# Sixteen-batch attention and FFN on one core: the down products of batches 13 and 14 computed one stage later

## The chip, the cores and the metric

The kernel runs on one core of a Trainium2 chip. The metric is the device time of one execution in microseconds (us); lower is better. TensorE is called PE here, VectorE DVE, ScalarE ACT, GpSimd POOL, and the queue of SyncE, which issues nearly all transfers, SP.

## The reference

For x of 16 batches, 512 tokens and 512 channels, in float32, one transformer layer with a layernorm ahead of and behind each half:

```python
x = x + layernorm(attention(layernorm(x), Wq, bq, Wk, bk, Wv, bv, Wo, bo))
x = x + layernorm(ffn(layernorm(x), gate_w, up_w, down_w, gate_s, up_s, down_s))

# attention: 32 heads of 16 channels, rotary turns, causal softmax
q, k, v = heads(x @ Wq.T + bq), heads(x @ Wk.T + bk), heads(x @ Wv.T + bv)
weights = softmax(where(causal, rope(q) @ rope(k).T / sqrt(16), -inf))
out = merge(weights @ v) @ Wo.T + bo

# ffn: 1408 inner channels, weights of -1, 0 and 1
g = (x @ gate_w.T) * gate_s
u = (x @ up_w.T) * up_s
out = ((silu(g) * u) @ down_w.T) * down_s
```

## The kernel before

**Stages.** The batches are handled one after another. A stage belongs to the attention of one batch b and has 8 groups of four heads with 6 steps each, 48 steps (`batches`, L910; `one_step`, L751). In every step PE computes scores of the current group (into the tile `st`, which ACT turns into weights `pt` with an exp, and POOL masks with an `affine_select`), and scores of the next group or the one after it (into the tiles `s`, from which DVE takes the maxima). Products of weights and values (`av`) follow in step 3 of a group and in step 0 of the next; their copy by ACT is `ot`. The tile `st` has one buffer in PSUM, `s` two, which is what one step fills. DVE turns the maxima round through PE (`pm`) and DMAs put them into `mx` (L615).

**What fills the steps.** Between these, each step takes a part of a list of other work. `dense` (L494) lists, for the next batch, the products of v, q and k, and for the batch before, the output product of the attention (`po`, `o_block`, L362), its two layernorms, and the transposes of the result (`px`, `turn`, L254). `ffn_list` (L706) lists the FFN of the batch before: 11 times a gate and an up product (`pg`, `pu`, L404), then for each of four blocks of 128 tokens a down product (`pd`, L429), and between these the first layernorm and transposes of the batch after the next. `merge` and `laid` (L468, L473) place follow-up work a given number of units behind a product; `run_list` (L693) spreads the list over the 48 steps by the units of its items (1 for a float32 product of 512 columns, 0.27 for one of the gate, up and down products, 0.15 for a transpose). So in stage 15 the list has the work of no next batch; L518 sets an item of 28 units that does nothing at its head. Each engine takes its instructions strictly in the order that the program writes them.

**Splits.** On the path that runs here (`self.exact`), the left operands of the gate, up and down products are parts of a float32 value, a rounded one and the rest, so each of these products comes twice. For the down product ACT copies four columns of blocks of `ht` into `hh`, and POOL computes the rest, `hl` (`split`, L458). Each has two buffers, and a down product of a block is 22 matmuls in three chunks (8, 8 and 6), each with a split of its own. In `ffn_list`, the split of chunk k of block tb + 1 is written behind chunk k of block tb, so its buffer is freed by the chunk that comes after it.

**The way of the heads.** When a group is done, `ot` goes to DRAM (`od`); after every second group, `sums` (L675) reads the sums and the values back (tiles `sum` and `oc`), DVE takes the reciprocal, it goes to DRAM (`rd`) and comes back repeated (tile `xr`), and POOL multiplies `oc` by it. `oc` has four buffers, one for each of the four pieces of 128 channels of a batch; `xr` has two, which also carry the residual x that `load_xr` (L390) reads.

**The end.** After stage 15 eight steps finish the attention (with no other work), and then L927 writes the rest of batch 15 in one piece: output product, layernorms, transposes, gate, up and down.

Of the kernel before, what the change touches and what calls it, by code (L numbers as in the profile page):

```python
# [18 lines left out]
P = 128  # L19
T = 512  # L20
C = 512
# [32 lines left out]
class Block:  # L54
# [15 lines left out]
    def __init__(self, tc, ctx, a):  # L70
        self.tc, self.a = tc, a
        nc = self.nc = tc.nc
        self.pe = InOrder(tc, nc.tensor)
        self.dve = InOrder(tc, nc.vector)
        self.act = InOrder(tc, nc.scalar)
        self.pool = InOrder(tc, nc.gpsimd)
        self.sp = InOrder(tc, nc.sync)
        self.B = a["x"].shape[0]
        self.F = a["wd"].shape[0]
        self.NF = self.F // P  # L80
        pool = lambda name, **k: ctx.enter_context(tc.tile_pool(name=name, **k))
        self.const = pool("const", bufs=1)
        self.work = pool("work", bufs=2)
        self.small = pool("small", bufs=5)
        self.dram = pool("dram", bufs=1, space=bass.MemoryType.DRAM)
        self.ps_s = pool("ps_s", bufs=2, space=bass.MemoryType.PSUM)
        self.ps_t = pool("ps_t", bufs=1, space=bass.MemoryType.PSUM)
        self.ps_av = pool("ps_av", bufs=1, space=bass.MemoryType.PSUM)
        self.ps_d = pool("ps_d", bufs=3, space=bass.MemoryType.PSUM)
        self.todo = defaultdict(list)  # L90
        self.step = 0
        self.exact = False
        for name in "xts xns xnts x1s x2ts ks qs mxs nms pts avs ots ocs rcs wts hts wfs yas xrs pieces".split():
            setattr(self, name, {})
        self.constants()
# [266 lines left out]
    def o_block(self, b, tb):  # L362

        st = {}

        def tail(p):
            x1 = st["x1"] = self.tile([P, C], "x1", bufs=4)
            self.dve.tensor_tensor(x1, p, self.row["bo"], ALU.add)
            st["mr"] = self.stats(x1)

        def rest_1():
            x1 = self.x1s[b, tb] = st["x1"]
            self.scaled(x1, x1, st["mr"])
            self.pool.tensor_tensor(x1, x1, self.xrs.pop((b, tb)), ALU.add)
            if tb + 2 < NB:
                self.load_xr(b, tb + 2)

        def rest_2():
            st["mr"] = self.stats(st["x1"])

        def rest_3():
            xn = self.tile([P, C], "xn", bufs=2)
            self.scaled(xn, st["x1"], st["mr"])
            self.xns[("f", b), tb] = xn

        return self.product(
            "po", NC, lambda c: self.ocs[b, c][:, ts(tb, P)], lambda c: self.wts[b, "o", c // 2][:, c % 2, :], tail
        ), rest_1, rest_2, rest_3
# [102 lines left out]
                waiting.remove(w)  # L491
        return out + [(0, w[1]) for w in waiting]

    def dense(self, b):  # L494


        L = []
        nxt, old = b + 1 < self.B, b >= 1
        o, bn = b - 1, b + 1
        do = lambda f, *args: L.append((0, lambda: f(*args)))  # L500

        def qk(name, c):
            items, rest, store = self.qk_block(bn, name, c)
            L.extend(items)
            self.merge(L, rest, 3)
            self.merge(L, store, 5.5)

        if nxt:
            for tb in range(NB):
                L += self.v_block(bn, tb)  # L510
            for c in range(NC):
                if c < 2:
                    do(self.load_w, o, "o", c)
                qk("q", c)
                if c % 2:
                    do(self.load_w, bn, "k", c // 2)
        elif b < self.B:
            L.append((28 * MM, lambda: None))  # L518
        if not nxt:
            for half in range(2):  # L520
                do(self.load_w, o, "o", half)
        later = []
        if old:
            do(self.load_xr, o, 0)
            do(self.load_xr, o, 1)
            for tb in range(NB):
                items, *rests = self.o_block(o, tb)
                L += items
                for r, k in zip(rests, (3.5, 6.5, 9.5)):
                    if r is rests[2] and tb >= 2:  # L530
                        later.append(r)
                    else:
                        self.merge(L, r, k, ("f", tb))
        for c in range(NC):
            if old:
                if c < 2:
                    do(self.load_wf, o, c)
                L.append(("need", ("f", c)))
                L += self.turn(self.xns, ("f", o), c, self.xnts, "xntf")
                if c < 2:  # L540
                    self.merge(L, later[c], 5, ("f", c + 2))
            if nxt:
                qk("k", c)
        return L
# [102 lines left out]
    def values(self, n, third):  # L647
        b, g = divmod(n, NG)
        if third == 0:
            self.avs[n] = self.ps_av.tile([P, T], FP, tag="av", name="av")  # L650
        av = self.avs[n]
        for kb, at, w in ST_SETS[third]:
            for j in range(4):
                h = 4 * g + j
                pt = self.pts[n, third, j // 2]
                pt = pt[:, j // 2, T // 2 * (j % 2) :] if third == 2 else pt[:, j % 2, :]
                self.pe.matmul(
                    av[32 * j : 32 * j + 32, T - w : T],
                    self.v17[b % 2][:, kb, h * W : h * W + 32],
                    pt[:, at : at + w],  # L660
                    start=(kb == 0),
                    stop=(third == 2),
                )
        for pair in range(2):
            del self.pts[n, third, pair]
        if third == 2:
            del self.ks[n], self.qs[n], self.mxs[n]
            ot = self.tile([P, T], "ot", bufs=1)
            self.act.copy(ot, self.avs.pop(n))
            i = (b % 2) * NC + g // 2  # L670
            self.later(1, lambda: self.sp.dma_start(out=self.od[i][P * (g % 2) : P * (g % 2) + P, :], in_=ot))
            if g % 2:
                self.later(2, self.sums, b, g // 2)

    def sums(self, b, c):  # L675
        i = (b % 2) * NC + c
# [26 lines left out]
                i += 1  # L703
            yield

    def ffn_list(self, o, nxt2):  # L706

        L = []
        do = lambda f, *args: L.append((0, lambda: f(*args)))
        NK = (self.NF + 3) // 4  # L710
        for f in range(self.NF if o is not None else 0):
            if f + 2 < self.NF:
                do(self.load_wf, o, f + 2)
            L += self.gate_up(o, f)
            if self.exact and (f % 4 == 3 or f == self.NF - 1):
                do(self.split, o, 0, f // 4)
            if nxt2 is not None:
                if 3 <= f < 7:
                    do(self.load_w, nxt2, "vq"[(f - 3) // 2], (f - 3) % 2)
                elif 7 <= f < 9:  # L720
                    do(self.load_x, nxt2, f - 7)
        if o is None:
            for tb in range(2):
                do(self.load_x, nxt2, tb)
            for k in range(4):
                do(self.load_w, nxt2, "vq"[k // 2], k % 2)
        for tb in range(NB):
            if nxt2 is not None:
                st = {}

# [2 lines left out]

                do(first)
                self.merge(L, lambda st=st: st["rest"](), 4, ("a", tb))
            if o is not None:
                items, rest, store = self.down(o, tb)
                if self.exact and tb + 1 < NB:
                    for k in range(NK):
                        L += items[8 * k : 8 * k + 8]  # L740
                        do(self.split, o, tb + 1, k)
                else:
                    L += items
                self.merge(L, rest, 4)
                self.merge(L, store, 8)
            if nxt2 is not None:
                L.append(("need", ("a", tb)))
                L += self.turn(self.xns, ("a", nxt2), tb, self.xnts, "xnta")
        return L

    def one_step(self, work, n, i):  # L751
        for f, args in self.todo.pop(self.step, []):
# [157 lines left out]
    def batches(self):  # L910
# [5 lines left out]
                self.one_step(work, n, i)  # L916
        for b in range(B):
            if b:
                L = self.dense(b) + self.ffn_list(b - 1, b + 2 if b + 2 < B else None)
                work = self.run_list(L, NG * STEPS)  # L920
            for g in range(NG):
                for i in range(STEPS):
                    self.one_step(work, b * NG + g, i)

        for i in range(STEPS + 2):
            self.one_step(iter(()), B * NG + i // STEPS, i % STEPS)
        for _, f in self.laid(self.dense(B) + self.ffn_list(B - 1, None)):  # L927
            f()


# [59 lines left out]
```

## Time and profile before

| | |
|---|---|
| time, median of 3 runs | 3273.52 us (3272.84 to 3274.5) |
| the profiled execution, its own time | 3268.2 us |
| its span, first to last instruction | 3266.5 us |
| mean granted PE clock | 0.973 |
| matmuls recorded | 21258 |
| bytes read and written in HBM | 345.79 MB, 125.30 MB |
| stage 13, from the last `ot` of batch 12 to the last of batch 13 | 191.3 us |
| stage 14, the same of batches 13 and 14 | 197.5 us |
| stage 15, the same of batches 14 and 15 | 188.4 us |
| from there to the first gate product of batch 15 | 49.2 us |
| from there to the end | 76.4 us |

How to read it: the profile is of one execution. Its busy times are sums over the instructions of an engine; matmuls overlap, so that the sum of their durations says less than the distance of their starts. The clock is the share of full speed that PE was granted. A wait is written as the waiting engine and group, an arrow, and what ended the wait, then us in total, times, and the longest. A stage is measured from the `ot` copy of the last group of one batch to that of the next, where the records show a stage's start and end best.

### The profile page before, as it was taken

What the parts mean: (1) busy time and instruction counts of PE and PEld (TensorE: products, weight loads), DVE (VectorE), ACT (ScalarE), POOL (GpSimd) and SP (SyncE); (2) the same over time, 40 slices, a digit from 0 to 9 for tenths busy, and PEclk for the clock granted to TensorE, in tenths of its full rate; (3) what the DMA queues carried; (4) which work ended last, traced back from release to release, by engine and by line L of the source; (5) the groups of instructions that cost most, each with busy time, mean ns of one, the idle gap of its engine ahead of it and who ended that gap; (6) DMA issues with size and microseconds to landing.
All of it is one profiled execution on the core that took longest, in us unless ns stands there. A gap on an engine that the chain in (4) does not pass through costs nothing. (4 is left out here: it accounts for less than half of the span.)

```text
span 3266.5 us, 59287 instructions
## 1 busy us (share of the span) xinstructions
PE 3110.4 (95%) x21258; PEld 1751.5 (54%) x21258; DVE 1888.5 (58%) x5911; ACT 1543.1 (47%) x2243; POOL 1383.4 (42%) x1933
## 2 busy tenths in 40 slices
PE   6889999999999999999999999999999999997868
PEld 2334655646455564645556464555646555463536
DVE  5455656565565656556565665656656565655522
ACT  5354545454454545445454545545454554543332
POOL 4143345453444545344454434445442544533142
PEclk9889999999999999999999999999999999997988
DMA  6454525345352534535244453535445353433321
GB/s 250 162 165 151 192 96 177 128 147 167 127 194 91 178 130 148 171 125 190 98 163 135 153 176 124 181 105 163 137 150 167 127 182 107 146 116 104 105 79 66
DMA packets 227441, 471.41 MB, mean 144 GB/s; under 512 B 40976, under 2 KB 45072, under 8 KB 226704
## 3 DMA queue, kind: packets, MB, share of 16 engines
q1 hardware_dynamic: 226704, 466.47, 42.9%
q8 instruction: 170, 2.79, 0.3%
q10 hardware_dynamic: 432, 1.05, 0.1%
q14 instruction: 135, 1.11, 0.1%
HBM read 345.79 MB, written 125.30 MB: 144 GB/s over the span
## 5 line engine op out<-in xcount | busy, mean ns | idle before, releaser
L49 DVE CUSTOM_DVE_ANT_0 s<-s,mask 128x512 f32<-128x512 f32 (+1 forms) x2034 | 974.8, 510 | 715.1 <-PE s L49 534.8
L49 ACT ACTIVATE pt<-st 128x1024 f32<-128x1024 f32 (+1 forms) x768 | 677.0, 881 | 753.3 <-PE st L49 742.7
L49 POOL TENSOR_SCALAR_AFFINE_SELECT pt<-pt 128x256 f32<-128x256 f32 (+1 forms) x768 | 392.7, 511 | 1200.9 <-ACT pt L49 1198.4
L49 PEld LDWEIGHTS st<-q,kh 32*128 32x128 f32 x2048 | 193.2, 185 | 473.7 <-issue 229.9
L49 PE MATMUL st<-q,kh 32*128 32x512 f32 (+3 forms) x2048 | 414.9, 401 | 31.3 <-ACT pt L49 29.8
L49 PE MATMUL s<-kh,q 32*128 32x512 f32 (+1 forms) x2034 | 415.9, 402 | 15.8 <-DVE nm L49 8.1
L49 PE MATMUL s<-kl,q 32*128 32x512 f32 (+1 forms) x2034 | 344.8, 324 | 11.5 <-DMA kl<-kd 11.4
L49 PE MATMUL st<-mx,one 2*128 2x512 f32 (+3 forms) x2048 | 335.9, 324 | 5.3 <-DMA mx<-nml 5.3
L49 PE MATMUL av<-pt,v 128*32 128x512 f32 (+3 forms) x4096 | 338.7, 449 | 0.0
L49 PE MATMUL st<-q,kl 32*128 32x512 f32 (+3 forms) x2048 | 336.5, 325 | 0.0
L49 POOL TENSOR_TENSOR hl<-ht,hh 128x512 fp32r<-128x512 f32 (+1 forms) x192 | 229.7, 1196 | 199.8 <-ACT hh L49 191.2
L49 DVE DVE_READ_ACCUMULATOR2_ANT nm<- 128x1 f32 x2048 | 289.4, 141 | 0.0
L49 PE MATMUL pd<-wd,hl 128*128 128x512 f32 x704 | 286.8, 407 | 2.0 <-POOL hl L49 2.0
L49 PE MATMUL pg<-xntf,wf 128*128 128x512 f32 x704 | 287.0, 408 | 1.3 <-ACT xntf L49 1.3
L49 PE MATMUL pd<-wd,hh 128*128 128x512 f32 x704 | 287.9, 409 | 0.0
L49 PE MATMUL pu<-xntf,wf 128*128 128x512 f32 x704 | 284.2, 404 | 0.0
L49 PE MATMUL pu<-xntfl,wf 128*128 128x512 f32 x704 | 284.0, 403 | 0.0
L49 PE MATMUL pg<-xntfl,wf 128*128 128x512 f32 x704 | 281.0, 399 | 0.0
L49 PE MATMUL po<-w,oc 128*128 128x512 f32 x512 | 245.4, 613 | 16.5 <-DMA w<-in_wo 16.5
L49 PE MATMUL pq<-xnta,w 128*128 128x512 f32 x480 | 239.7, 631 | 6.1 <-ACT xntf L49 5.4
L49 PE MATMUL pk<-xnta,w 128*128 128x512 f32 x480 | 240.2, 619 | 3.9 <-DVE ya L49 3.9
L49 ACT CAST hh<-ht 128x512 fp32r<-128x512 f32 (+1 forms) x192 | 111.9, 583 | 272.9 <-PE pd L49 215.3
(118 smaller groups left out, 5086.8 us busy)
## 6 DMA issues: line engine op xcount, KB each, us to landing
wf<-wgs SPq DMA_DIRECT2D x176, 512.0 KB
q<-qd SPq DMA_DIRECT2D x128, 256.0 KB
kh<-kd SPq DMA_DIRECT2D x128, 256.0 KB
kl<-kd SPq DMA_DIRECT2D x128, 256.0 KB
od<-ot SPq DMA_DIRECT2D x128, 256.0 KB
w<-in_wo SPq DMA_DIRECT2D x34, 512.0 KB
xr<-in_x SPq DMA_DIRECT2D x66, 256.0 KB
w<-in_wq SPq DMA_DIRECT2D x32, 512.0 KB
```

The source lines that it names most:

```text
L49: return self.tc.keep_in_program_order(f(*args, **kwargs))
```

## The change

`ffn_list` becomes two functions, `gate_ups` and `downs`. For batches up to 12 the order stays as it was. The down products of batch 13 leave stage 14 and go into stage 15: blocks 0 and 1 at the head of its list, where the empty item was, and blocks 2 and 3 between the output products of batch 14 and the transposes behind them. Those of batch 14 leave stage 15: blocks 0 and 1 go into the eight steps that finish the attention, block 2 behind three of the four pieces of the output products of blocks 0 and 1 of batch 15, and block 3 behind all output products. Both halves of the output weights of batch 15 are requested at the start of these eight steps.

In these moved products a split is written behind the product that frees its buffer: behind chunk 0 the split of chunk 2 of the same block, behind chunks 1 and 2 those of chunks 0 and 1 of the next block.

Since `x1` (four buffers) then holds blocks of two batches at once, three blocks take a tile of `x` instead, and the second layernorm's result of blocks 2 and 3 of the last two batches takes one of `sg`. The transfers of `sums` for the first three pairs of groups of batch 14 come 8 steps after the group instead of 2.

```diff
+        self.spare = [(self.B - 2, 2), (self.B - 2, 3), (self.B - 1, 3)]
...
-            x1 = st["x1"] = self.tile([P, C], "x1", bufs=4)
+            tag, bufs = ("x", 2) if (b, tb) in self.spare else ("x1", 4)
+            x1 = st["x1"] = self.tile([P, C], tag, bufs=bufs)
...
-            xn = self.tile([P, C], "xn", bufs=2)
+            xn = self.tile([P, C], "sg" if b >= self.B - 2 and tb >= 2 else "xn", bufs=2)
...
-    def dense(self, b):
+    def dense(self, b, between=()):
...
-        elif b < self.B:
-            L.append((28 * MM, lambda: None))
-        if not nxt:
+        else:
             for half in range(2):
                 do(self.load_w, o, "o", half)
...
-                    if r is rests[2] and tb >= 2:
+                    if r is rests[2] and tb >= 2 and nxt:
                         later.append(r)
                     else:
                         self.merge(L, r, k, ("f", tb))
+        L += between
...
-                self.later(2, self.sums, b, g // 2)
+                self.later(8 if b == self.B - 2 and g < NG - 1 else 2, self.sums, b, g // 2)
...
+    def gate_ups(self, o, nxt2, apart=False):
...
-            if self.exact and (f % 4 == 3 or f == self.NF - 1):
+            if self.exact and (f in (3, 7) or f == self.NF - 1 and not apart):
                 do(self.split, o, 0, f // 4)
...
+    def downs(self, o, nxt2, tbs=range(NB), apart=False, late=False):
...
+            items, rest, store = self.down(o, tb)
+            if self.exact and late:
+                for k in range(NK):
+                    L += items[8 * k : 8 * k + 8]
+                    if k == 0:
+                        do(self.split, o, tb, 2)
+                    elif tb + 1 < NB:
+                        do(self.split, o, tb + 1, k - 1)
+            elif self.exact and tb + 1 < NB:
+                for k in range(NK):
+                    L += items[8 * k : 8 * k + 8]
+                    do(self.split, o, tb + 1, k)
...
+    def last_list(self):
+        L = []
+        do = lambda f, *args: L.append((0, lambda: f(*args)))
+        o = self.B - 1
+        for tb in range(2):
+            do(self.load_xr, o, tb)
+        blocks = [self.o_block(o, tb) for tb in range(NB)]
+        n = NC - 1
+
+        def rests(tb):
+            for r, k in zip(blocks[tb][1:], (2.5, 5, 7.5)):
+                self.merge(L, r, k, ("f", tb))
+
+        for tb in range(2):
+            L += blocks[tb][0][:n]
+        L += self.downs(o - 1, None, (2,), True, True)
+        for tb in range(NB):
+            L += blocks[tb][0][n if tb < 2 else 0 :]
+            rests(tb)
+        for f in range(2):
+            do(self.load_wf, o, f)
+        L += self.downs(o - 1, None, (3,), True, True)
+        for tb in range(NB):
+            L.append(("need", ("f", tb)))
+            L += self.turn(self.xns, ("f", o), tb, self.xnts, "xntf")
+        return L + self.gate_ups(o, None) + self.downs(o, None)
...
             if b:
-                L = self.dense(b) + self.ffn_list(b - 1, b + 2 if b + 2 < B else None)
+                if b < B - 1:
+                    L = self.dense(b)
+                    L += self.gate_ups(b - 1, b + 2 if b + 2 < B else None, b + 2 == B)
+                    if b < B - 2:
+                        L += self.downs(b - 1, b + 2)
+                else:
+                    down = [self.downs(b - 2, None, tbs, True, True) for tbs in ((0, 1), (2, 3))]
+                    L = down[0] + self.dense(b, down[1]) + self.gate_ups(b - 1, None, True)
                 work = self.run_list(L, NG * STEPS)
...
-
+        L = [(0, lambda half=half: self.load_w(B - 1, "o", half)) for half in range(2)]
+        work = self.run_list(L + self.downs(B - 2, None, (0, 1), True, True), STEPS + 2)
         for i in range(STEPS + 2):
-            self.one_step(iter(()), B * NG + i // STEPS, i % STEPS)
-        for _, f in self.laid(self.dense(B) + self.ffn_list(B - 1, None)):
+            self.one_step(work, B * NG + i // STEPS, i % STEPS)
+        for _, f in self.laid(self.last_list()):
             f()
```

More of the change, by code (lines that the diff above doesn't have):

```diff
@@ L539, in dense @@
                 L += self.turn(self.xns, ("f", o), c, self.xnts, "xntf")
-                if c < 2:
+                if c < len(later):
                     self.merge(L, later[c], 5, ("f", c + 2))
@@ L704, in run_list @@
             yield
-    def ffn_list(self, o, nxt2):
+    def gate_ups(self, o, nxt2, apart=False):
         L = []
         do = lambda f, *args: L.append((0, lambda: f(*args)))
-        NK = (self.NF + 3) // 4
-        for f in range(self.NF if o is not None else 0):
+        for f in range(self.NF):
             if f + 2 < self.NF:
@@ L721, in ffn_list @@
                     do(self.load_x, nxt2, f - 7)
[L722 to L727, printed above, removed]
+        return L
+    def downs(self, o, nxt2, tbs=range(NB), apart=False, late=False):
+        L = []
+        do = lambda f, *args: L.append((0, lambda: f(*args)))
+        NK = (self.NF + 3) // 4
+        if self.exact and apart and not late and 0 in tbs:
+            do(self.split, o, 0, 2)
+        for tb in tbs:
             if nxt2 is not None:
@@ L735, in ffn_list @@
                 self.merge(L, lambda st=st: st["rest"](), 4, ("a", tb))
[L736 to L745, printed above, removed]
+            items, rest, store = self.down(o, tb)
[11 more added lines that the diff above has]
+            else:
+                L += items
+            self.merge(L, rest, 4)
+            self.merge(L, store, 8)
             if nxt2 is not None:
@@ L749, in ffn_list @@
         return L
+    def last_list(self):
+        L = []
+        do = lambda f, *args: L.append((0, lambda: f(*args)))
+        o = self.B - 1
[19 more added lines that the diff above has]
+        return L + self.gate_ups(o, None) + self.downs(o, None)
     def one_step(self, work, n, i):
@@ L918, in batches @@
             if b:
-                L = self.dense(b) + self.ffn_list(b - 1, b + 2 if b + 2 < B else None)
+                if b < B - 1:
[3 more added lines that the diff above has]
+                        L += self.downs(b - 1, b + 2)
+                else:
+                    down = [self.downs(b - 2, None, tbs, True, True) for tbs in ((0, 1), (2, 3))]
+                    L = down[0] + self.dense(b, down[1]) + self.gate_ups(b - 1, None, True)
                 work = self.run_list(L, NG * STEPS)
```

## The prediction

> **What bounds the kernel now.** First the page: TensorE (PE) is the busiest engine, and the slices show where it isn't busy.
>
> ```profile
> PE 3110.4 (95%) x21258; PEld 1751.5 (54%) x21258; DVE 1888.5 (58%) x5911; ACT 1543.1 (47%) x2243; POOL 1383.4 (42%) x1933
> ...
> PE   6889999999999999999999999999999999997868
> ...
> PEclk9889999999999999999999999999999999997988
> ```
>
> PE is full but at the start and in the last four slices. So second, the busy time by stage, cut where the output copy `ot<-av` of the last group of batches 13, 14 and 15 starts (2755.0, 2952.5, 3140.9) and at the last FFN's first product (3190.1). Columns after the stretch and its length: busy us of PE, weight loads, DVE, ACT, POOL; granted clock; DMA share.
>
> ```profile
> 2755.00:2952.00 197.00, 189.30 (x1306) 105.83 (x1306) 112.08 (x354) 90.21 (x131) 81.48 (x111) 0.99 0.40 128
> 2952.00:3141.00 189.00, 159.21 (x1149) 94.85 (x1149) 88.14 (x277) 71.93 (x103) 61.34 (x96) 0.86 0.29 97
> 3141.00:3190.00 49.00, 19.60 (x48) 9.20 (x48) 13.05 (x32) 9.05 (x13) 13.95 (x22) 0.68 0.29 97
> 3190.00:3266.50 76.50, 64.96 (x264) 50.87 (x264) 23.41 (x39) 17.69 (x28) 22.41 (x24) 0.92 0.21 70
> ```
>
> Stage 14 is PE-bound. Stage 15 idles 30 us, the gap after it 29 us, both at a lowered clock. Third, PE's waits from 2949 to 3190 name who is late:
>
> ```profile
> PE px L49 <- ACT xn L49: 26.1, 7, 5.7
> PE po L49 <- DMA w<-in_wo: 16.5, 1, 16.5
> PE st L49 <- ACT pt L49: 8.7, 8, 2.4
> PE st L49 <- DMA mx<-nml: 5.3, 1, 5.3
> PE s L49 <- DMA kh<-kd: 2.0, 1, 2.0
> ```
>
> The 26.1 us are the two layernorm chains (of batch 14 in stage 15, of 15 after it), with nothing between output product and transposes. The 16.5 us are the serial way of the last heads through DRAM (od, sum, rd, xr, then the weights w). The rest falls into the first part of stage 15, where 28 units of the list are an empty item. Fourth, the clock there:
>
> ```profile
> 2952.00:2956.00 4.00, 1.43 (x12) 0.78 (x12) 1.40 (x4) 2.09 (x3) 1.80 (x3) 0.71 0.52 154
> ...
> 2964.00:2968.00 4.00, 3.24 (x28) 1.43 (x20) 1.84 (x9) 1.15 (x2) 1.04 (x2) 0.50 0.19 65
> ```
>
> Unfilled attention runs at half clock. But from 3040 to 3137, with 9 products in each step, PE is busy 97.00 of 97.00 us at 1.00.
>
> **What the Trainium skill says.** "TensorE: Matmul & The Clock Gate", HAM oscillation: idle gaps over about 3.4 us make the clock fall to half. The trace agrees: 0.50 here, and the last FFN's first products start 0.43 us apart (from 3191.4), later ones 0.2265. "PSUM — Partial Sum Buffer", Engine vs sequencer instructions: ACT, DVE and POOL are strict FIFO, matmuls keep program order. So a split that waits on ACT for its buffer holds the exps behind it; in the last Downs `hh` waits 13.6 us for `pd`. "DMA: Bandwidth & Descriptors", Latency and other measured facts: some 2 us of fixed cost each; here od 2.27, sum 2.11, rd 2.32 us in the chain.
>
> **The change part by part.** PE's work is only moved: 2 x 88 `pd` products.
>
> *Prices at full clock.* Starts in the timeline from 3056 to 3078: scores of a step 0.90, 1.06 or 0.55 us (two steps of each in a group), values 1.43 and 0.99, `pm` 0.12: 7.56 us a group. Gate and up 8 in 1.81 us, so 0.2265 each; `pd` 0.234 (2941.7 to 2944.3); `po` 0.86 (two records of 0.43); four transposes 0.60 to 0.65. Check: the group from 3056.8 to 3078.0 took 21.2 us and held 54 gate/up products: 12.2 + 7.56, and 1.4 left over, for changing between streams twice a step. I keep 1.4 a group.
>
> *Stage 14 loses four Downs*: 88 x 0.234 = 20.6 us of bound PE time. The 48 steps stay, now with some 2.1 us of other work instead of 2.5; an exp takes 1.03 us and still hides. 197.5 becomes 177 (172 if its stalls, such as 1.3 us of `pk` on DVE `ya`, thin out; 181 if thinner steps add some). **-20.5 us.**
>
> *Stage 15* takes the Downs of batch 13 (two ahead of the output products, two between these and the transposes) for those of batch 14, and the empty item goes. The built order shows seven products, or two `po`, in nearly every step. Work: 88 x 0.234 = 20.6; 16 x 0.86 = 13.8; transposes 2.5; 176 x 0.2265 = 39.9; attention 8 x (7.56 + 1.4) = 71.7. Sum 148.5. Added waits:
> - The output weights are queued on SP behind the loads of the next group (q, kh, kl, 768 KB); before, they came ahead of them (issued 2979.4, first used 2984.8). At the 330 GB/s of 2984 to 2988, 1.28 MB is 3.9 us; add 1.8 us of issue. PE gets to `po` some 3.3 us after the issue starts: 2.5 us (0 to 6). Behind `po` on PE stands all later attention.
> - Reductions of the 128/384 scores end 2.1 us after the scores (3060.6 to 3062.7), and only two score buffers exist. Seven products and `pm` cover 1.9 us; with a gate/up tail ahead (0.69 to 0.75) it is late: 0.4 x 8 = 3 us (0 to 8).
> - Splits come behind the product that frees their buffer. ACT isn't blocked (gain, under 2 us), but a split's 0.62 + 1.29 us, behind an exp and an `affine_select`, has one chunk to hide in: 24 chunks, mostly hidden, 3 us (0 to 6). In both cases the late product or score holds the rest of PE's order.
>
> 148.5 + 8.5 = 157, against 188.4: **-31.4 us** (150 to 167). The layernorm chain of 14 (some 8 us a block; 3182.6 to 3188.3 shows its second half) lies under two Downs, 10.3 us plus attention.
>
> *Other moves.* Four stores of `y` go from stage 14's end to stage 15's start on SP, ahead of `mx` and the group loads: each waits for POOL `y`, and is placed 8 units after its product, 4 steps, when `y` is long done: 0. POOL and ACT get the splits where they were 33% and 38% busy: 0. The sums of groups 1, 3, 5 of batch 14 come 6 steps later, since `oc` reuses batch 13's tiles, read now in steps 13 to 20 of the stage instead of 11 to 16; without it SP would hang with the group loads behind: 0. In stage 15 that same wait (9.7 us on `po`, then `mx` late, the 5.3 us) shrinks, since `po` ends in step 14, when the sums start. `x` and `sg` tiles lent to blocks 2 and 3 are free by then: 0.
>
> *After stage 15*, from that `ot` to the first gate product, PE now has 39 `pd`, 6 `po` (three of four pieces of two blocks, no last heads needed), 22 `pd`, 10 `po`, 22 `pd`, 16 transposes. In the last FFN 88 `pd` with splits took 23.5 us, 0.267 each; so 10.4 + 5.2 + 5.9 + 8.6 + 5.9 = 36. The way through DRAM took 14.3 us (3140.9 to 3155.2); before `po` needs it lie 21.5 us: hidden, and the weights are asked for ahead of it. The last block's chain (8 us, and 3 for sharing POOL) outlasts the last Down and twelve transposes by 3.3 us; with these (1.8), the last transposes (0.65) and the copy to the product (1.2) it is 43 to 44. Against 49.2: **-5.2 us** (-8 to -1).
>
> *Last FFN*: its first 13 products lost 13 x 0.2 = 2.6 us at half clock. A shorter gap may or may not keep it: **-1.5** (0 to -3).
>
> Sum: -20.5 - 31.4 - 5.2 - 1.5 = -58.6. The profiled execution took 3268.2 (span 3266.5 and 1.7 around it), so 3209.6. The median, 3273.5, lies 5.3 above; I take the same for the changed kernel: **3215**.
>
> **The rivals.**
> - *Everything packs* (10%): best ends of all four, -25.5 - 38.4 - 8 - 3 = -75: 3199. For: 97 us without a gap. Against: thinner steps, DVE's tail.
> - *Thin steps* (15%): seven products don't cover the loop of scores, exp and reductions, and a group takes the 20.6 us of the unfilled one (2952.5 to 2973.1): 8 x 20.6 + 2.5 = 167.5. With 177, and 2 us in all after stage 15: -20.5 - 20.9 - 2 = -43: 3230. Against: the 20.6 were at half clock.
> - *The stall moves* (5%): weights, sums or a lent tile arrive late in stage 15 or after it, 10 us in each of three places: -28: 3245.
> - *Slower* (3%): small waits keep the clock half down in stages 14 and 15. Their PE work at 1.00 is 189.3 - 20.6 = 169 and 148.5, so 317 us. At a mean clock of c it takes 317/c; the whole gain is eaten when 317 x (1/c - 1) = 59, below c = 0.84. At 0.80 the loss is 79: 3294. Against: 0.86 was stage 15's mean with 35 us of nearly nothing to do.
> - The change does what it says: the built order shows the moved products.
>
> **How the numbers follow.** Likeliest (67%): 3215, own range 3204 to 3226. The range for 8 in 10 takes in most of the packed case and of the thin one: 3199 to 3235. Faster by over 0.2% (6.5 us, about what a measurement of this kernel tells from none): 0.67 + 0.10 + 0.15 + 0.05 = 0.97, less 0.01 for smaller gains: 0.96; same 0.01; slower 0.03.
>
> **What would show it.** Stage 14 at 177 us from `ot` to `ot`; stage 15 at 157, groups of 18 to 20 us, clock near 1.00; no `po` wait for w over 6 us; `px` waits under 8 us in all instead of 26.1; 43 to 44 us from the last `ot` to the first `pg`. Wrong if groups of stage 15 stay over 20 us, if PE waits long for kh, kl or mx there, or if the clock stays under 0.9.

## The result, and the profile after

The changed kernel took 3216.24 us (median of 4 runs, 3209.38 to 3220.06) against 3273.18 us before: a ratio of 0.9825, with a 95% interval of 0.9807 to 0.9843. In a second set of runs, on the chip of the first experiments, it took 3223.83 against 3273.55 us, 0.985 (0.9833 to 0.9868). The forecast was 3215.

The page's rows for the whole execution, after:

```profile
span 3214.0 us, 59287 instructions
...
PE 3097.9 (96%) x21258; PEld 1743.3 (54%) x21258; DVE 1888.0 (59%) x5911; ACT 1542.7 (48%) x2243; POOL 1383.9 (43%) x1933
...
PE   6889999999999999999999999999999999999988
...
PEclk9899999999999999999999999999999999999999
```

The same instructions, and the hole of the last four slices is nearly gone. By stage, cut at the same events as before (the last `ot` of batches 13, 14 and 15, and for the end of the third row the first gate product); the columns are as in the prediction:

```profile
2756.24:2928.20 171.96, 168.13 (x1231) 90.12 (x1235) 105.47 (x338) 82.45 (x117) 64.46 (x92) 1.00 0.44 146
2928.20:3088.94 160.74, 152.49 (x1148) 89.57 (x1149) 86.84 (x277) 70.80 (x102) 60.98 (x95) 0.96 0.35 115
3088.94:3138.59 49.65, 39.75 (x131) 25.36 (x130) 19.63 (x49) 17.15 (x27) 30.93 (x42) 0.90 0.25 85
```

Stage 14 gave 25.5 us, stage 15 27.7, the stretch after it nothing (49.2 became 49.7), though it took in 83 more products (the other five of batch 14's 88 ran just ahead of it); PE is busy there for 39.8 us instead of 19.6. The last FFN gave 0.9. That is 53.6; the spans differ by 52.5, since stage 14 began 1.2 us later. Such shifts arise in the earlier stages, which the change leaves alone: the last `ot` of batch 12 came at 2563.7 before, 2565.6 after, and 2568.9 in a second profile of the changed kernel, while its stages 14 and 15 then took 172.1 and 161.9. So the experiments are read by these lengths, and the times only beside them.

PE's waits from 2740, shortly before stage 14, to the end, after:

```profile
PE pd L49 <- POOL hl L49: 9.2, 10, 2.8
PE po L49 <- DMA w<-in_wo: 3.7, 1, 3.7
PE pd L49 <- ACT hh L49: 2.2, 1, 2.2
PE s L49 <- DVE nm L49: 1.8, 4, 0.5
PE pg L49 <- ACT xntf L49: 1.5, 2, 0.8
```

The old heads of this list, px with 26.1 us and po with 16.5, are gone or small. A new one leads: the moved Downs (down products) wait for their splits, for all but the 1.5 us that the last FFN has of it.

### The profile page after: what moved, and what is told of

Same layout as the page of the kernel before. It is cut to its first block, busy times and chain, and to the rows that moved or that the text cites. A ratio compares the mean times of both kernels' runs of the same rounds, so it can differ in the third digit from the quotient of the medians.

```text
span 3214.0 us, 59287 instructions
## 1 busy us (share of the span) xinstructions
PE 3097.9 (96%) x21258; PEld 1743.3 (54%) x21258; DVE 1888.0 (59%) x5911; ACT 1542.7 (48%) x2243; POOL 1383.9 (43%) x1933
## 4 chain that ended last, share of the span: by engine, by line
PE 83%; DVE 2%; DMA 2%; ACT 2%; POOL 1%; issue 1%; SPq 0%; ACTq 0%; DVEq 0%; POOLq 0%
PE st L49 16%; PE pu L49 11%; PE pg L49 10%; PE av L49 9%; PE pd L49 9%; PE po L49 7%; PE pq L49 6%; PE pv L49 5%; PE pk L49 5%; PE s L49 3%; DMA kl<-kd 2%; PE px L49 1%; ACT pt L49 1%; DVE s L49 1%; PE pm L49 1%
## 5 line engine op out<-in xcount | busy, mean ns | idle before, releaser
L49 PE MATMUL st<-q,kh 32*128 32x512 f32 (+3 forms) x2048 | 411.2, 398 | 22.3 <-ACT pt L49 20.9
L49 POOL TENSOR_TENSOR yl<-ya,yh 128x512 fp32r<-128x512 f32 x128 | 163.3, 1276 | 169.4 <-ACT yh L49 169.4
```

What stands on the lines that cost most here:

```text
L49: return self.tc.keep_in_program_order(f(*args, **kwargs))
```

## The experiments

Each variant is of the changed kernel unless it says otherwise. The ratio is to the kernel before on the same chip; there were three chips. Each stage length is read from one profile. "End" is the time from the last `ot` to the first gate product.

| variant | ratio to before, interval | stage 14 | stage 15 | end | last FFN |
|---|---|---|---|---|---|
| before | 1 | 197.5 | 188.4 | 49.2 | 76.4 |
| changed | 0.9825 (0.9807 to 0.9843) | 172.0 | 160.7 | 49.7 | 75.5 |
| changed, again | 0.985 (0.9833 to 0.9868) | 172.1 | 161.9 | 49.9 | 75.3 |
| weights_early | 0.9806 (0.979 to 0.9822) | 172.1 | 154.1 | 51.9 | 73.8 |
| batch13_only | 0.9887 (0.9869 to 0.9905) | 172.7 | 175.1 | 50.2 | 75.2 |
| late_splits_everywhere | 0.9897 (0.9878 to 0.9916) | 173.7 | 157.6 | 50.3 | 75.3 |
| no_cover | 0.9881 (0.9864 to 0.9899) | 174.0 | 175.9 | 49.8 | 75.2 |
| sum_later | 0.984 (0.9819 to 0.9861) | 174.0 | 160.7 | 46.7 | 75.6 |
| chunk_early | 0.9829 (0.9812 to 0.9847) | 174.2 | 158.7 | 52.0 | 76.0 |
| output_first | 0.9799 (0.9782 to 0.9816) | 171.9 | 161.7 | 48.5 | 73.9 |
| adds_on_dve | 0.9834 (0.9807 to 0.9861) | 174.0 | 163.3 | 51.8 | 74.1 |
| all_four | 0.9813 (0.9791 to 0.9835) | 172.3 | 154.4 | 49.4 | 74.0 |
| warm_filler, of before | 1.0 (0.9987 to 1.0012) | 197.5 | 188.0 | 49.3 | 76.4 |
| short_empty, of before | 1.0004 (0.999 to 1.0018) | 198.4 | 189.7 | 49.6 | 75.2 |

How much of such a length is chance can be read where the program of a stage is the same. Stage 14 is written alike in the changed kernel and all its variants, and took 171.9 to 174.2 us. Stage 15 is written alike in seven of these profiles (both of the changed kernel, late_splits_everywhere, sum_later, chunk_early, output_first, adds_on_dve) and took 157.6 to 163.3 us, 160.7 in the mean. The end is written alike in five (both of the changed kernel, weights_early, late_splits_everywhere, no_cover) and took 49.7 to 51.9. The last FFN, alike but for lent tiles in all but the two with additions on DVE, took 73.8 to 76.4. A difference within these ranges means nothing without a wait that names it.

**The changed kernel once more.**

> The changed kernel as it is, to be compared with the variants on one chip. Both theories: 53 to 60 us under the kernel before, so 3213 to 3220, with some 172 us of stage 14 and 160 us of stage 15 from output copy to output copy.

It came out at 3223.83, slower than expected by 4 us, with the stages as expected. In its profile most of the shift lies ahead of stage 13, which begins 3.4 us later than in the first profile.

**Is it the products that fill holes, or the clock that is kept up?** First only batch 13's Downs moved:

> Only the Downs of batch 13 are put off; those of batch 14 stay at stage 15's end, and what comes after stage 15 is as before the change. Filling theory (a moved product counts its own 0.234 us where it is taken from, and nothing where it fills a hole): stage 14 as in the changed kernel, 172; stage 15 20.6 us longer than there, so 181; after it 49 to 50 us; in all 20 us more than the changed kernel, 33 to 36 less than before. Clock theory (what counts is that PE's clock is kept up through stage 15 and after; the products themselves are small): within 8 us of the changed kernel in stage 15, and loss only after it.

```diff
-                    L = down[0] + self.dense(b, down[1]) + self.gate_ups(b - 1, None, True)
+                    L = down[0] + self.dense(b, down[1]) + self.gate_ups(b - 1, None) + self.downs(b - 1, None)
...
```

The eight last steps are empty again, and the end is written as before the change. Stages 14 and 15 of this variant:

```profile
2753.85:2926.52 172.67, 168.68 (x1233) 90.52 (x1237) 105.62 (x338) 82.97 (x119) 65.47 (x93) 1.00 0.46 146
2926.52:3101.58 175.06, 164.46 (x1228) 101.66 (x1228) 94.23 (x293) 77.94 (x115) 78.25 (x115) 1.00 0.32 104
```

Stage 15 is 14.3 us longer than in the changed kernel, not 20.6, with 12 us more of busy PE. So neither expectation holds as it stands: at a full clock, even above the 0.96 of the changed kernel, the stage is longer, but by less than the price of its products. The missing 6 us are, by the profile, the wait for the output weights `w` and the low clock behind it. With more work in the list, each step takes more of it, and the weights are asked for ahead of the loads of the next group, where the changed kernel asks behind them. SP in this variant, then in the changed kernel:

```profile
2937.90 0.91 SPq L49 DMA_DIRECT2D w<-in_wo  x2
...
2946.05 0.84 SPq L49 DMA_DIRECT2D q<-qd  x1
```

```profile
2942.09 0.33 SPq L49 DMA_DIRECT2D q<-qd  x1
...
2943.73 2.56 SPq L49 DMA_DIRECT2D w<-in_wo  x2
```

`po` waits 0.2 us for `w` here instead of 3.7, and the first group takes 22.9 us at full clock instead of 25.9. Beside weights_early below, where that wait is gone too, stage 15 is 21.0 us longer (175.1 and 154.1), near the 20.6: in a full stage the products count at their full price. The end, without 83 of the products, is no shorter than with them. Batch 13's part alone is worth 25 + 13 us (with the wait for `w` gone), batch 14's some 14.

Second, the empty item of the kernel before with useless products in it:

> The kernel before, with its empty item of 28 units replaced by 70 products of constants that nobody reads, six or so in a step, so that no Down moves. If the half clock of the unfilled steps costs what I think: the first two groups of stage 15, 20.6 and 19.4 us, take 17 to 18 us each at full clock in spite of 16 us of useless work, and the kernel gets 3 to 6 us faster. If those groups were bound by the loop of scores and exp, whatever the clock: 3 to 12 us slower.

```diff
-            L.append((28 * MM, lambda: None))
+            for k in range(70):
+
+                def warm():
+                    p = self.psum("pz")
+                    self.pe.matmul(p, self.one, self.wd[:, 0, :], start=True, stop=True)
+
+                L.append((0.4, warm if self.exact else lambda: None))
```

The first two groups of stage 15 in this variant, then in the kernel before:

```profile
2961.74:2982.50 20.76, 17.89 (x154) 10.94 (x154) 8.66 (x34) 6.00 (x9) 5.05 (x9) 1.00 0.40 129
2982.50:3001.00 18.50, 18.50 (x154) 10.30 (x152) 9.71 (x35) 6.01 (x8) 2.90 (x6) 1.00 0.42 144
```

```profile
2952.49:2973.11 20.62, 14.25 (x117) 7.45 (x117) 8.66 (x34) 6.00 (x9) 5.04 (x9) 0.53 0.41 130
2973.11:2992.51 19.40, 16.35 (x125) 7.92 (x129) 9.80 (x36) 6.01 (x9) 2.90 (x6) 0.71 0.42 137
```

Both expectations miss. The clock rises from 0.53 and 0.71 to 1.00, and some 15 us of products come in (64 of the 70, at 0.23); yet the two groups take 39.3 us instead of 40.0. What the clock alone gave and what the products alone took isn't separated; together they are nothing. Over the whole of stage 15 the mean clock rises from 0.86 to 0.94 and the length stays (188.0 and 188.4). So a raised clock doesn't account for the gain, and the free room is shown directly.

Third, half of the empty item cut:

> The kernel before, with the empty item cut from 28 units to 12 (what the last heads need to arrive), the same work spread over more steps, no Down moved. Filling theory: six of twelve empty steps go, with their idle time and half clock: stage 15 takes 8 to 12 us less than 188.4, the layernorm chain (px, some 12 us) and what comes after stay. That much of the gain would then need no moved product. If the rest gets thinner steps and is bound by other loops: within 3 us of before.

```diff
-            L.append((28 * MM, lambda: None))
+            L.append((12 * MM, lambda: None))
```

The expectation of 8 to 12 us less fails, the other one (within 3 us) holds: stage 15 takes 189.7. Its first, third and the last three groups:

```profile
2958.47:2985.10 26.63, 18.61 (x123) 8.76 (x127) 8.67 (x34) 6.00 (x10) 5.02 (x9) 0.55 0.47 160
...
3004.90:3044.30 39.40, 25.74 (x169) 15.88 (x169) 17.10 (x52) 13.29 (x20) 9.41 (x17) 0.70 0.40 131
...
3083.50:3105.60 22.10, 22.10 (x178) 14.25 (x174) 13.86 (x43) 8.46 (x13) 3.41 (x7) 1.00 0.05 19
3105.60:3130.10 24.50, 21.86 (x127) 14.07 (x127) 3.99 (x10) 9.53 (x17) 13.80 (x18) 0.86 0.12 36
3130.10:3148.10 18.00, 14.61 (x103) 9.06 (x101) 3.44 (x8) 8.21 (x13) 11.08 (x15) 1.00 0.16 58
```

PE still idles 27.7 us of the stage (29.2 before): 8.0 in the first group, 13.7 in the third, under the bare layernorm chain, and 6.0 in the last two. There the Downs have splits in the old order: `hh` waits 24.6 us on ACT for `pd` (13.4 before the change), and from 3100 on `st` waits 3.8 us for exps. Here, spreading the same work only moves the holes; other work filled them.

**What covers the layernorm chain?**

> The changed kernel, with all four Downs of batch 13 at the head of stage 15's list, none between batch 14's output products and their transposes (the sums of batch 15's first three pairs then come later too, as their tiles are still being read). Filling theory: the layernorm chain lies bare again, px waits some 12 us as before the change, and stage 15 takes 10 to 15 us more, 171 to 176. If the attention that runs beside it would cover the chain: within 3 us of 161.

```diff
-                    L = down[0] + self.dense(b, down[1]) + self.gate_ups(b - 1, None, True)
+                    L = down[0] + down[1] + self.dense(b) + self.gate_ups(b - 1, None, True)
...
-                self.later(8 if b == self.B - 2 and g < NG - 1 else 2, self.sums, b, g // 2)
+                self.later(8 if b >= self.B - 2 and g < NG - 1 else 2, self.sums, b, g // 2)
```

PE's waits in stage 15 of this variant:

```profile
PE px L49 <- ACT sg L49: 11.1, 2, 5.7
PE po L49 <- DMA w<-in_wo: 4.7, 1, 4.7
PE pd L49 <- POOL hl L49: 2.1, 3, 1.4
PE px L49 <- ACT xn L49: 1.6, 1, 1.6
```

175.9 us, 14 to 15 more than the two profiles of the changed kernel: px waits 12.7 us again. The two Downs between are the cover, as the filling theory had it.

**The wait for w.** In the changed kernel, SP asks for q, kh and kl at 2942.1 to 2943.1, then for w; PE reaches po at 2945.6. From the timeline after:

```profile
2943.73 2.56 SPq L49 DMA_DIRECT2D w<-in_wo  x2
...
2949.26 2.08 PE L49 MATMUL po<-w,oc 128*128 128x512 f32 x2 [3.70 <-DMA w<-in_wo]
```

> The changed kernel with both halves of batch 14's output weights asked for at the head of stage 15's list instead of just ahead of the output products. If the 3.7 us wait of po for w, and the half clock of the 8 us after it, come from the place of these two requests behind the group loads: no such wait, 5 to 6 us less than the changed kernel, all of it in the first two groups of stage 15. If the two requests only change what the transfers collide with (the group loads then arrive late): within 2 us of it, with waits for kh or kl in their place.

```diff
-        else:
-            for half in range(2):
-                do(self.load_w, o, "o", half)
...
-                    L = down[0] + self.dense(b, down[1]) + self.gate_ups(b - 1, None, True)
+                    w = [(0, lambda half=half: self.load_w(b - 1, "o", half)) for half in range(2)]
+                    L = w + down[0] + self.dense(b, down[1]) + self.gate_ups(b - 1, None, True)
```

Stage 15 of this variant, and its first group here and in the changed kernel:

```profile
2926.84:3080.93 154.09, 147.73 (x1148) 87.33 (x1149) 86.85 (x277) 70.68 (x102) 60.94 (x95) 0.99 0.36 116
...
2926.84:2946.50 19.66, 18.28 (x156) 10.95 (x156) 11.88 (x42) 9.55 (x15) 11.82 (x15) 1.00 0.38 121
```

```profile
2928.20:2954.12 25.92, 20.85 (x156) 11.49 (x156) 11.78 (x42) 9.56 (x15) 13.86 (x18) 0.89 0.37 124
```

6.6 us less than in the changed kernel, and no waits for w, kh or kl in its first three groups. The first group takes 19.7 us instead of 25.9; the wait was 3.7 of the 6.3, and the slowed clock behind it most of the rest: PE was busy 2.6 us longer with the same products. This version takes 3209.77 us, 14 less than the changed kernel on the same chip; by the profiles, what of it isn't in stage 15 lies where the edit changes nothing.

**Do the late splits help?** By the order of the program, the old order can't be had in the moved Downs: behind the second Down, a split of the third block would stand on ACT until products ran that come after steps whose exps stand behind this split; nothing would end. No run shows this. Instead the late order went everywhere:

> The changed kernel, with the splits of all batches' moved and unmoved Downs up to 13 behind the product that frees their buffer, as only the last two full FFNs have it. If splits that wait on ACT hold up PE: 13 stages each gain 1 to 3 us, 13 to 40 us in all. If they are hidden by the fuller steps of these stages, as I think: within 6 us, either way.

```diff
-                    L += self.gate_ups(b - 1, b + 2 if b + 2 < B else None, b + 2 == B)
+                    L += self.gate_ups(b - 1, b + 2 if b + 2 < B else None, True)
                     if b < B - 2:
-                        L += self.downs(b - 1, b + 2)
+                        L += self.downs(b - 1, b + 2, range(NB), True, True)
```

It lies 15 us above the changed kernel, outside both expectations. PE's waits from 500 us to the last `ot` of batch 12, first of this variant, then of the changed kernel:

```profile
PE pd L49 <- POOL hl L49: 13.9, 22, 0.9
PE s L49 <- DMA kl<-kd: 11.9, 10, 2.3
PE pm L49 <- DVE ya L49: 5.5, 11, 0.8
```

```profile
PE s L49 <- DMA kl<-kd: 9.5, 10, 2.5
PE st L49 <- ACT pt L49: 6.7, 23, 0.4
PE pm L49 <- DVE ya L49: 5.2, 11, 0.5
```

The late order does free the exps: the 23 waits of `st` are gone. But it asks for a split one chunk later, and 22 waits of `pd` come in their place, at twice the time. The last `ot` of batch 12 comes at 2583.2 instead of 2565.6 (2561.3 to 2572.7 in all profiles with the old order). These two kinds of wait account for 7 of the 17.6 us; the rest is not settled.

**The end.** Two stalls stand in it. The first, after:

```profile
3093.69 0.35 DVE L49 RECIPROCAL sum<-sum 128x32 f32<-128x32 f32 x1 [6.67 <-DMA sum<-od]
3093.96 0.63 DVE L49 TENSOR_TENSOR y<-pd,dscale 128x512 f32<-128x512 f32 x1
...
3095.80 0.56 POOL L49 TENSOR_TENSOR ln_rstd<-ln_ve,neghalf 128x1 f32<-128x1 f32 x1 [2.43 <-DVE ln_ve L49]
3096.45 0.26 POOL L49 TENSOR_SCALAR ln_sh<-ln_mv,ln_rstd 128x1 f32<-128x1 f32 x1
3096.68 1.26 POOL L49 TENSOR_TENSOR hl<-ht,hh 128x512 fp32r<-128x512 f32 x1
...
3097.99 0.50 PE L49 MATMUL pd<-wd,hl 128*128 128x512 f32 x1 [2.45 <-POOL hl L49]
```

Read upwards: pd waits for hl, hl stands on POOL behind two scalars of a layernorm, these wait for DVE's statistics of y, and y stood on DVE behind a reciprocal that waited for a transfer.

> The changed kernel, with the reciprocal of the very last heads (and the two transfers behind it) written one step later. DVE takes its instructions in order, and the reciprocal stood until 3093.7 on the transfer of the sums, with the Down's tail behind it, then POOL's layernorm scalars, then hl. If that row of queues is why pd waits 2.45 us for hl at 3095.5: that wait is under 0.5 us, and from the last output copy to the first gate product it takes 47 to 48 us instead of 49.7. If POOL is simply short of time there: no change, within 0.5 us.

```diff
-        self.later(1, self.sums_2, b, c, s)
+        self.later(2 if (b, c) == (self.B - 1, NC - 1) else 1, self.sums_2, b, c, s)
```

The end takes 46.7 us instead of 49.7, 0.3 better than the expected 47 to 48, and 3.0 below the shortest of the five ends that are alike. The waits left in it are 4.7 us for hl and 2.2 for hh.

The second stall, after:

```profile
3127.09 0.80 ACT L49 ACTIVATE xn<-x,ln_sh,ln_rstd 128x512 f32<-128x512 f32 x1
3127.26 1.27 POOL L49 TENSOR_TENSOR x<-x,xr 128x512 f32<-128x512 f32 x1 [0.77 <-ACT x L49]
3127.79 0.49 ACT L49 CAST hh<-ht 128x384 fp32r<-128x384 f32 x1
3128.34 0.50 PE L49 MATMUL pd<-wd,hh 128*128 128x512 f32 x1 [2.20 <-ACT hh L49]
...
3130.61 1.00 POOL L49 TENSOR_TENSOR hl<-ht,hh 128x384 fp32r<-128x384 f32 x1
...
3131.66 0.79 PE L49 MATMUL pd<-wd,hl 128*128 128x512 f32 x1 [2.83 <-POOL hl L49]
```

Here the split stands behind the layernorms of batch 15 on ACT and POOL. Three tries:

> The changed kernel, with the first chunk of the last moved Down (and with it the last split) ahead of the output products of blocks 2 and 3, where the layernorm work isn't yet in ACT's and POOL's queues. If the two waits of pd at 3126 to 3131.7 (2.2 us for hh, 2.8 us for hl) come from the last split standing behind layernorm work in these queues: both go, but the last block's layernorm then ends last; from the last output copy to the first gate product 47 us instead of 49.7 (46 to 48). If the layernorm chain alone sets the end there: no change, within 0.7 us.

```diff
         for tb in range(NB):
+            if tb == 2:
+                L += items[:8]
+                do(self.split, o - 1, 3, 2)
             L += blocks[tb][0][n if tb < 2 else 0 :]
             rests(tb)
         for f in range(2):
             do(self.load_wf, o, f)
-        L += self.downs(o - 1, None, (3,), True, True)
+        L += items[8:]
+        self.merge(L, rest, 4)
+        self.merge(L, store, 8)
```

(`items, rest, store = self.down(o - 1, 3)` stands ahead of it.) The wait for hh went, and this came:

```profile
PE px L49 <- ACT sg L49: 4.9, 1, 4.9
```

A second wait of this kind follows it, 8.4 us in both: the last block's chain now ends last. 52.0 us is 2.3 more than in the changed kernel, but the unchanged end once took 51.9: no gain, and whether it is a loss stays open. Neither expectation holds.

> The changed kernel, with all output products of batch 15 in one piece behind the first two moved Downs, and the other two Downs behind all of them, so that 44 products lie under the layernorm chain instead of 22 (the last block keeps its tile in x1). If the chain of the last block sets the end: 45 to 46 us from the last output copy to the first gate product instead of 49.7. If it is the splits that stand behind layernorm work: more of them do so now, the waits of pd for hh and hl grow from 8 us to 10 or more, and it is 50 us or longer.

```diff
-        self.spare = [(self.B - 2, 2), (self.B - 2, 3), (self.B - 1, 3)]
+        self.spare = [(self.B - 2, 2), (self.B - 2, 3)]
...
-        n = NC - 1
-
-        def rests(tb):
+        for tb in range(NB):
+            L += blocks[tb][0]
             for r, k in zip(blocks[tb][1:], (2.5, 5, 7.5)):
                 self.merge(L, r, k, ("f", tb))
-
-        for tb in range(2):
-            L += blocks[tb][0][:n]
-        L += self.downs(o - 1, None, (2,), True, True)
-        for tb in range(NB):
-            L += blocks[tb][0][n if tb < 2 else 0 :]
-            rests(tb)
         for f in range(2):
             do(self.load_wf, o, f)
-        L += self.downs(o - 1, None, (3,), True, True)
+        L += self.downs(o - 1, None, (2, 3), True, True)
```

48.5 us. The wait for hh (2.2 us) is gone, but in the end pd now waits 8.6 us for hl, where it waited 6.2 in the changed kernel: 8.6 us for splits instead of 8.4. Neither expectation holds; the waits only changed their place. The variant's median, 3211.14 us, gives the lowest ratio of the table, but the profiled execution is the slowest of its four (3220.95), and its end and last FFN are only 2.7 us shorter than the changed kernel's. What else it gained isn't traced.

> The changed kernel, with the residual additions of batch 15's output blocks and of the Downs of batches 14 and 15 on DVE (0.69 us each) instead of POOL (1.27 us). If POOL's queue, with splits and layernorm in it, sets the end of what comes after stage 15: 46 to 47 us there instead of 49.7, and 1 to 2 us less in the last FFN. If the chain of the last block is long by its number of steps and not by that queue: 49 us.

```diff
-            self.pool.tensor_tensor(x1, x1, self.xrs.pop((b, tb)), ALU.add)
+            (self.dve if b == self.B - 1 else self.pool).tensor_tensor(x1, x1, self.xrs.pop((b, tb)), ALU.add)
...
-            self.pool.tensor_tensor(y, y, self.x1s.pop((b, tb)), ALU.add)
+            (self.dve if b >= self.B - 2 else self.pool).tensor_tensor(y, y, self.x1s.pop((b, tb)), ALU.add)
```

51.8 us, again no more than the unchanged end once took. In it pd waits 9.3 us for hl instead of 6.2, the longest 4.6. Most additions were shorter (0.69 us), but DVE's queue, which all statistics go through, now had them in it. The last FFN took 74.1 us; weights_early and output_first have 73.8 and 73.9 with the additions on POOL, so that isn't their doing. Less work on POOL alone doesn't shorten the end. That the order sets it in which chains that depend on each other stand in three queues is shown at one place, by sum_later; for the rest it is my reading.

> The changed kernel with the weights asked for early (7 us less in stage 15), the later reciprocal (3 us less after it), all output products in one piece ahead of the last two moved Downs, and the residual additions of the end on DVE. If the gains add: stage 15 154, after it 43 to 44 instead of 49.7, the last FFN 73 to 74; 14 to 16 us less than the changed kernel. If they overlap: 9 to 11 us less.

(The edits are those above together.) Stage 15 takes 154.4, as with the early weights alone, but the end 49.4, with 6.3 us of waits for hl and 2.3 for hh: the gains of the end don't add. The ratio of 0.9813 (3212.64 us) isn't better than the 0.9806 of the early weights alone; it is some 12 us under the changed kernel's 0.985, near the 9 to 11 expected if the gains overlap. What order of these queues would let the end run at PE's pace stays open.

## Why the prediction was right, step by step

The sum was -58.6 and the profile has -53.6 in the same four terms. One term was too small and three too large.

- *Stage 14*, -20.5 forecast, -25.5 measured. Busy PE fell by 21.1 (189.3 to 168.1), near the forecast's 20.6. The other 4.4 us is idle time (8.2 before, 3.8 after), which I had allowed for as the low end.
- *Stage 15*, 157 forecast, 160.7 measured. The mechanism holds: the layernorm chain is covered (no_cover: 15 us), the room was free (warm_filler: 15 us). The step mis-sized is "2.5 us (0 to 6)" for the weights: the wait was 3.7, and I left out that the clock is low behind it (0.54 and 0.60 from 2948 to 2956). weights_early puts a number on the whole: 6.6. Without it the stage is at 154.1, so the other added waits cost 5.6, not 6. DVE's late maxima took 1.2 us, where I had 3; the splits 1.4 in one wait.
- *After stage 15*, -5.2 forecast, +0.5 measured. This is the step that failed. The way through DRAM is hidden, as forecast, and so is the wait for w. But 0.267 a product was read from a stretch where the queues hold the splits, the layernorms and the residual additions of the Downs themselves, and nothing else. Here the 39 products took 14.4 us instead of 10.4 (3089.0 to 3103.4), and the last 22 took 11.6 instead of 5.9 (3122.4 to 3134.0), with a reciprocal or the layernorms of batch 15's output blocks ahead of the splits on ACT, POOL and DVE; in both, part of it is half clock behind a wait. The 22 between took 5.5. "3 us for sharing POOL" was added to the chain only; the Downs pay too. sum_later takes 3.0 of it back. What earlier weights for batch 15 would give the old end by themselves wasn't run.
- *The last FFN*, -1.5 forecast, -0.9 measured. short_empty, where it is written as before, has 75.2 us in place of 76.4, so a change of this size shows nothing.
- *The rivals.* Thin steps: no; groups of gate and up took 18.1 to 18.6 us, 7.56 + 1.4 + 43 x 0.2265 = 18.7. (Its own 8 x 20.6 + 2.5 is 167.3, not 167.5.) Three groups did stay over 20 us, a sign of being wrong by the forecast's own list: the first (25.9) by its wait for w, the third and fourth (22.1 and 22.3) with PE all but full (idle for 1.0 and 1.9). Slower by the clock: no; 1.00 and 0.96 in the two stages. The stall moves: in part, 3.7 us for w, and in the end.
- The forecast called the late splits a small gain on ACT and 3 us of risk in stage 15. In full stages they cost some 1.5 us each; in the moved Downs, as argued above, they are what makes the order possible.
- *The half clock.* The forecast reads the 0.50 in the first groups of stage 15 as agreeing with the gaps of over 3.4 us that the Trainium skill names ("TensorE: Matmul & The Clock Gate", HAM oscillation). It doesn't: PE's longest wait from 2949 to 2992 was the 2.4 us of `st` in the forecast's list (the 5.3 us for mx came later), so here shorter waits, one after another, went with half the clock. The last FFN's slow start does come behind a wait of 5.7 us.

That the median fell on the forecast to 1 us is luck. For the profiled execution the forecast was 3209.6, and it took 3215.86: 6.3 us too low. To this it added 5.3 us, by which the median before lay above the profiled execution; after, the median lay 0.4 above. The two errors nearly cancel, and the four runs spread over 10.7 us.

## What to carry to other kernels

Work that is bound at one stage and free at another is worth moving by a stage: take each product at its full price where it leaves a full stage, and at nothing where the profile shows holes and useless products run free in them. Then price the rest of what moves: a request that slips behind others in a queue cost its wait and the slowed clock after it here (3.7 us of wait, 6.6 in all), and a product's helpers (here splits on ACT and POOL) wait behind whatever else stands in their queues at the new place. Don't count on spreading holes away: in this kernel thinner steps only shifted them.

## What was not expected of the hardware

Filling PE's holes with 70 useless products raised the granted clock from 0.53 and 0.71 to 1.00 in two groups, and left their length where it was (40.0 and 39.3 us). So in these steps, which wait on other engines, half a clock was a sign of room; whether a full clock without the products would have shortened them isn't shown. It did cost something where dense products followed a wait: `av` and `po` after the 3.7 us wait, the products from 3098.6 to 3100.7 at 0.43 us each after one of 2.45 us, and before the change the first 13 products of the last FFN.
